# Moving the maximum's injection and the second value half within a turn, with a first attention that copies less on VectorE

## The chip, the cores and the metric

The kernel runs on one core of one Trainium2 chip. Its time is the device time of one launch in microseconds. One profiled execution gives the trace that all durations come from.

## The reference, cut to what matters

The input is 16 sequences of 256 tokens with 128 channels, in fp32. A first attention layer (16 heads of 8 channels, windows of 64 tokens, no look-back) is added to the input; then six layers of a local transformer (16 heads of 64 channels, windows of 32 tokens that also see the window before) follow on its normalised result.

```python
x = x + first_attention(layernorm(x))           # qkv, layernorm of q and k per head, softmax over 64 keys, projection
h = layernorm(x)
for i in range(6):
    a = shift_tokens(h)                          # half of the channels come from the token before
    q, k, v = split(a @ Wqkv[i])                 # 128 -> 3 x 1024
    q, k = rotary(l2norm(q) * qs), rotary(l2norm(k) * ks)
    p = softmax(8 * q @ k.T, masked to the own and the preceding window)
    h = h + (p @ v) @ Wo[i]                      # 1024 -> 128
    h = h + ffn(shift_tokens(h))                 # layernorm, 128 -> 2 x 341, a * gelu(gate), 341 -> 128
x = x + h
```

## The kernel before, in words

**First attention.** `first_attention` works on eight units of 512 tokens. Each passes through six stages (`stage_load`, `stage_qkv`, `stage_heads`, `stage_soft`, `stage_out`, `stage_norm`), and a loop over 25 steps puts the stages of several units side by side; `merge` mixes their pieces by offsets. `row_stats` takes the mean and the spread of a row with ScalarE activations that accumulate. `stage_heads` splits queries and keys into two fp16 parts (`hl`: a cast on ScalarE, the remainder on GpSimd), doubles them by a copy on VectorE, and transposes by DMA. `stage_out` multiplies probabilities with values for the two halves `c` of the rows, each half into a PSUM tile `po` of its own, divides on VectorE, and projects. `SPLIT0` gives the PSUM banks of the pools in the order `pq`, `ps`, `po`, `py`, `pt`.

**The six layers.** There are 192 tiles of 128 tokens, 32 in a layer, and the main loop makes one turn for each. A turn works on five tiles at once: the projections of tile t (`stage_p`: key halves K0 and K1, query halves Q0 and Q1, value halves V0 and V1, each three fp16 matmuls of 512 columns), the scores of t-1 (`stage_s`), the softmax of t-2 (`stage_e`), the product with the values of t-3 (`stage_v`, in two halves `mb`, below called v0 and v1) and the output product of t-5 (`stage_w`). Between a projection's matmuls stand four fp32 transposes on TensorE (`turned`): of K and Q of t-1 beside K0 to Q1, of the probabilities of t-2 beside V0 and V1. ScalarE copies four of them at a time out of PSUM. A piece of the feed-forward (`stage_f`) of an earlier group of four tiles is added to a turn.

**What sets the order.** Every stage is a generator, and `AT_*` gives the place of each of its pieces in a turn, from 0 to 1. `merge_at` sorts them, with ties going to the part that was appended first. Every matmul and transpose is pinned behind the one before (`pin`), so TensorE runs exactly in the written order. The other engines' orders come from the framework's scheduler at build time, and stand then: each engine runs its instructions in that order.

```python
AT_P = tuple(c / 6 for c in range(6))
AT_E, AT_V, AT_W, AT_S = (0.2, 0.21), (0.1, 0.45), (0.47,), (0.72,)
SPLIT = (2, 4, 2)
USE = dict(p=0, t=1, w=1, f=1, s=2)
USE_V = (1, 2)
```

So the order of a turn on TensorE before is K0, v0, K1, injection, Q0, v1, w, Q1, V0, scores, V1, with the feed-forward's pieces in between.

**The softmax.** The scores open with a mask matmul (`rowsb`, `maskb`) into two PSUM tiles, one for each parity `a` of the head, and stay in PSUM. VectorE takes their negated maxima (`nm`, L738). In the next turn `stage_e` adds these with a matmul against an identity (`identh`), the maximum's injection, and ScalarE takes the exponentials (`p`, L275).

**PSUM.** `SPLIT` gives two banks to the projections, four to transposes, output product, feed-forward and v0, and two to scores and v1. The last two banks therefore go round within a turn: exponentials read them, v1 writes them, VectorE reads v1's result (`rc` L790, `of` L791), and the mask of the next scores writes them again.

**VectorE in a turn.** Four `mc` (L643, the rotary product of a projection of K or Q), four `r` (L653, the sum of the squares that ScalarE makes, L652), two `nm`, four `rc` and four `of` (two for each value half), two `xg` (L817, the output product added to the stream), and the feed-forward's and the weight splits' (L137) operations. ScalarE's square of a projection starts after VectorE's `mc` of the same bank.

**The end.** `emit_out` transposes a finished group back on TensorE, with PSUM from the projections' two banks, adds the first residual on VectorE (L834) and stores it.

Of the kernel before, what the change touches and what calls it, by code (L numbers as in the profile page):

```python
# [10 lines left out]
F32 = mybir.dt.float32  # L11
# [3 lines left out]
AF = mybir.ActivationFunctionType  # L15
ALU = mybir.AluOpType
AX = mybir.AxisListType
# [7 lines left out]
KT = 2  # L25
LAG_S, LAG_P, LAG_V, LAG_W = 1, 2, 3, 5
AT_P = tuple(c / 6 for c in range(6))
AT_E, AT_V, AT_W, AT_S = (0.2, 0.21), (0.1, 0.45), (0.47,), (0.72,)
AT_F = ((0.86,), (0.06, 0.74, 0.88), (0.03, 0.27, 0.8), (0.1, 0.35, 0.6))
AT_L = 0.71  # L30
LOAD_AT = 6
LOAD_T = 10
SPLIT = (2, 4, 2)
SPLIT0 = (2, 2, 2, 1, 1)
USE = dict(p=0, t=1, w=1, f=1, s=2)
USE_V = (1, 2)
LQ0, LH0, LS0, LO0, LN0 = 2, 4, 6, 7, 9
# [11 lines left out]
VPRE = 16.0  # L49
# [6 lines left out]
def kernel(  # L56
# [233 lines left out]
    def mul(*args, **how):  # L290
        pin(T.matmul(*args, **how))  # L291
# [5 lines left out]
    def first_attention(p1, p2, p3, pqp, psp0, pop, pyp, ptp=None):  # L297
# [17 lines left out]
        def row_stats(xt, pre):  # L315
            mu = p3.tile([128, 4], F32, name=f"{pre}mu")
            rs = p3.tile([128, 4], F32, name=f"{pre}rs")
            sq = p3.tile([128, 128], F32, name="sq0")
            for t in range(4):
                S.activation(sq, xt[:, t], AF.Copy, scale=-1.0 / 128.0, accum_out=mu[:, t : t + 1])  # L320
            for t in range(4):
                S.activation(sq, xt[:, t], AF.Square, bias=mu[:, t : t + 1], accum_out=rs[:, t : t + 1])
            rsqrt(rs, rs, 1.0 / 128.0)
            return mu, rs
# [39 lines left out]
        def stage_load(u):  # L364
            if u:
                load_x(u)
            e = U[u]
            _, e.rs = row_stats(e.xt, "a")
            e.rv = p1.tile([128, 4], F32, name="rv")
            V.tensor_scalar(e.rv, e.rs, VPRE, None, ALU.mult)  # L370
            yield
            e.xnt = p1.tile([128, 2, 4, 128], FR, name="xnt")
            pt = ptp.tile([128, 4, 128], F32, name="pt" if ptp is not pyp else "py")
            for t in range(4):
                T.transpose(pt[:, t], e.xt[:, t], ident)
            S.copy(e.xnt[:, 0], pt)
            V.tensor_tensor(e.xnt[:, 1], pt, e.xnt[:, 0].bitcast(F32), ALU.subtract)
            G.tensor_tensor(e.xt, e.xt, bpt.unsqueeze(1).to_broadcast([128, 4, 128]), ALU.add)
            yield
# [26 lines left out]
        def stage_heads(u):  # L406
            e = U[u]
            e.hl = []
            for s in range(2):
                src = e.qk[:, :, s * 128 : s * 128 + 128].rearrange("p t (h d) -> p t h d", d=8)  # L410
                hl = p1.tile([128, 4, 16, 4, 8], HP, name=f"hl{s}")
                for t in range(4):
                    hi, lo = hl[:, t, :, 0], hl[:, t, :, 2 if s else 1]
                    S.copy(hi, src[:, t])
                    G.tensor_tensor(lo, src[:, t], hi, ALU.subtract)
                    if s:
                        V.tensor_copy(hl[:, t, :, 1:4:2], hl[:, t, :, 0:3:2])
                    else:
                        V.tensor_copy(hl[:, t, :, 2:4], hl[:, t, :, 0:2])
                tr = p2.tile([128, 4, 4, 128], HP, name=f"tr{s}")  # L420
                nc.sync.dma_start_transpose(
                    tr.rearrange("p t i q -> p (t i) q"), hl.rearrange("p t h a d -> p (t h a d)")
                )
                e.hl.append(tr)
                yield
# [41 lines left out]
        def stage_out(u, n2):  # L467
            e = U[u]
            for n in range(2):
                t = 2 * n2 + n  # L470
                pt0 = e.pt[n]
                v = v0[(4 * u + t) % NV0]
                o0 = p3.tile([128, 2, 8, 8], F32, name="o0")
                for c in range(2):
                    r = slice(64 * c, 64 * c + 64)
                    po = pop.tile([128, 8, 18], F32, name="po")
                    for gm in range(8):
                        p = gm % 4 * 2 + gm // 4
                        for q, (a, b) in enumerate(((0, 0), (0, 1), (1, 0))):
                            T.matmul(po[:, p], pt0[r, a * 8 + gm], v[r, b, p], start=(q == 0), stop=(q == 2))  # L480
                    rc = p3.tile([128, 8], F32, name="rc0")
                    V.reciprocal(rc, po[:, :, 16])
                    for hp in range(2):
                        h = slice(64 * hp, 64 * hp + 64)
                        V.tensor_tensor(
                            o0[h, c],
                            po[h, :, hp * 8 : hp * 8 + 8],
                            rc[h].unsqueeze(2).to_broadcast([64, 8, 8]),
                            ALU.mult,
                        )  # L490
                yield
                py = pyp.tile([128, 512], F32, name="py")
                T.transpose(py[:, 0:128], o0.rearrange("p c a b -> p (c a b)"), ident)
                ot0 = p3.tile([128, 128], F32, name="ot0")
                S.copy(ot0, py[:, 0:128])
                py = pyp.tile([128, 512], F32, name="py")
                for c in range(2):
                    r = slice(64 * c, 64 * c + 64)
                    for hp in range(2):
                        T.matmul(  # L500
                            py[r, 0:128],
                            ot0[r, hp * 64 : hp * 64 + 64],
                            wp[r, hp],
                            start=(hp == 0),
                            stop=(hp == 1),
                        )
                V.scalar_tensor_tensor(e.xt[:, t], py[:, 0:128], 1.0 / VPRE, e.xt[:, t], ALU.mult, ALU.add)
                yield
# [49 lines left out]
    def bank(kind):  # L558
        n = USE.get(kind, kind)
        return banks[n].tile([128, 512], F32, name=f"bank{n}")  # L560
# [47 lines left out]
    def turned(src, dst, mb):  # L608
        hold = []

        def one(m):
            if m == 0:
                hold.append(bank("t").rearrange("p (m q) -> p m q", q=128))
            flip(hold[0][:, m], src(m), ident)
            if m == 3:
                to = dst
                if isinstance(dst, Tl):
                    if mb == 0:
                        dst.pt = work.tile([128, 8, 128], F32, name="pt", bufs=1)
                    to = dst.pt  # L620
                S.copy(to[:, mb * 4 : mb * 4 + 4], hold[0])  # L621

        turns.extend((lambda m=m: one(m)) for m in range(4))

# [63 lines left out]
    def line_up(t):  # L688
        if 0 <= t - LAG_S < total:
            d = tiles[t - LAG_S]  # L690
            if d.j == 0:
                kts[0] = front.tile([128, 8, 256], F32, name="kt", bufs=KT)
            d.ktp = kts[0]
            d.kt = d.ktp[:, :, 128 - 128 * d.j : 256 - 128 * d.j]
            d.qt = front.tile([128, 8, 128], F32, name="qt", bufs=2)
            for s, dst in ((1, d.kt), (0, d.qt)):
                for hb in range(2):
                    nat = d.nat[s][hb].rearrange("p (m a) d -> p m (a d)", a=2)
                    turned(lambda m, nat=nat: nat[:, m], dst, hb)
        if 0 <= t - LAG_P < total:  # L700
            d = tiles[t - LAG_P]
            for mb in range(2):
                turned(lambda m, mb=mb: d.p[:, mb * 4 + m].rearrange("p a k -> p (a k)"), d, mb)

# [60 lines left out]
    def stage_v(t):  # L765
        d = tiles[t]
# [11 lines left out]
        for mb in range(2):  # L778
            po = [bank(USE_V[mb])[:, 0:260].rearrange("p (m d) -> p m d", d=65) for a in range(2)]
            for m in range(4):  # L780
                for s in range(4):
                    for a in range(2):
                        r = slice(64 * a, 64 * a + 64)
                        q = slice(32 * s, 32 * s + 32)
                        mm = mb * 4 + m
                        mul(po[a][q, m], d.pt[r, mm, q], vv[s, a][r, mm], start=True, stop=True)
            of = work.tile([128, 4, 2, 64], F32, name="of", bufs=2)
            for a in range(2):
                rc = work.tile([128, 4], F32, name="rc", bufs=4)
# [30 lines left out]
    def emit_out(b, nb):  # L820
        g, k = divmod(b, GB)
        n = 2 * nb
# [4 lines left out]
        yt = pool.tile([128, 12 if name == "gt" else 4, 128], F32, name=name, bufs=bufs)[:, 0:n]  # L827
        for a in range(2):
            r = slice(64 * a, 64 * a + 64)
            pm = bank("p")[:, 0:256].rearrange("p (t c) -> p t c", c=64)[:, 0:n]  # L830
            for t in range(n):
                c0 = t % 2 * 128 + a
                flip(pm[:, t], xg[g][r, k + t // 2, c0 : c0 + 128], ident[r, r])
            V.tensor_tensor(yt[:, :, r], pm, r1[:, :, r], ALU.add)  # L834
# [187 lines left out]
```

## Time and profile before

| what | value |
|---|---|
| median of three runs | 3218.96 us (3212.57 to 3219.44) |
| the profiled execution | 3213.12 us, its span 3211.3 us |
| TensorE (PE) busy | 2994.2 us, 93% |
| VectorE (DVE) busy | 2583.3 us, 80% |
| GpSimd (POOL) busy | 2510.2 us, 78% |
| ScalarE (ACT) busy | 2384.4 us, 74% |
| mean granted TensorE clock | 0.957 |

Reading it: an engine's busy time counts its instructions and not its waits. PE is TensorE's matmuls and PEld its weight loads, which overlap them. Matmuls overlap each other, so the time that one takes of the engine is the time from its start to the next one's start, not its duration. In the list of waits a row names who waited, on whom, for how many microseconds in all, how often, and the longest. In the table of stages each row gives the stretch, its length, and for PE, PEld, DVE, ACT and POOL the busy time and the number of instructions; then the granted clock, the DMA engines' busy share and GB/s. In a timeline a row is start, length, engine, line, operation, tiles and count; in square brackets stands the idle time before it and what ended it.

### The profile page before, as it was taken

Reading aid. Unit: us, or ns where it says so; the run is one execution under the profiler, and the core shown is the slowest. Engines: PE = TensorE matmul, PEld = TensorE weight load, DVE = VectorE, ACT = ScalarE, POOL = GpSimd, SP = SyncE. Lnnn points to the kernel's source line nnn. Section 1 sums busy time; section 2 is a strip of 40 time slices with the busy share of each in tenths; the row PEclk is TensorE's granted clock in tenths of the full one; section 3 lists DMA queues with packets and bytes.
Section 4 is the critical chain, followed back from the end, with each engine's and each line's share of the span. In section 5 each row is a group of like instructions: output and inputs, shape, how many; then the busy total and the mean of one; then the engine's idle time right before and its main releaser. Section 6 shows DMA issues by size and latency. Waiting matters only on the chain. (4 is left out here: it accounts for less than half of the span.)

```text
span 3211.3 us, 153330 instructions
## 1 busy us (share of the span) xinstructions
PE 2994.2 (93%) x67106; PEld 2099.0 (65%) x67106; DVE 2583.3 (80%) x4850; ACT 2384.4 (74%) x5034; POOL 2510.2 (78%) x2578
## 2 busy tenths in 40 slices
PE   4887999999999999999999999999999999999997
PEld 3655766666666666666666666666666666666664
DVE  7987888887788887788887788887788887787774
ACT  6877777777777777777777777777777777776774
POOL 5656988888888788888788888788888788887772
PEclk6558999999999999999999999999999999999998
DMA  4763545444444434444444444444444444443433
GB/s 109 134 130 86 101 96 106 89 85 88 93 95 107 87 87 88 93 95 105 89 87 86 94 96 104 89 88 84 95 98 103 89 89 81 95 93 91 89 89 71
DMA packets 622945, 302.98 MB, mean 94 GB/s; under 512 B 533446, under 2 KB 545732, under 8 KB 622276
## 3 DMA queue, kind: packets, MB, share of 16 engines
q1 hardware_dynamic: 622276, 293.18, 43.5%
q8 instruction: 528, 8.65, 1.1%
q14 instruction: 141, 1.16, 0.1%
HBM read 22.45 MB, written 4.19 MB: 8 GB/s over the span
## 5 line engine op out<-in xcount | busy, mean ns | idle before, releaser
L291 PE MATMUL bank<-wqkv,xhl 128*128 128x512 f16 x3456 | 1234.4, 380 | 10.0 <-ACT sq L652 9.3
L654 POOL TENSOR_TENSOR sum<-mc 128x512 f32<-128x512 f32 x768 | 995.8, 1300 | 230.4 <-DVE mc L643 211.3
L643 DVE TENSOR_TENSOR mc<-bank,tq 128x1024 f32<-128x1024 f32 x768 | 928.2, 1218 | 148.3 <-PE bank L294 135.4
L664 POOL TENSOR_TENSOR sum<-sum,r 128x512 f32<-128x512 f32 x768 | 796.2, 1058 | 31.9
L653 DVE TENSOR_REDUCE r<-sq 128x8 f32<-128x512 f32 x768 | 520.4, 683 | 277.4 <-ACT sq L652 267.4
L294 PE MATMUL bank<-ident,sum 128*128 128x128 f32 x3072 | 710.5, 273 | 0.0
L796 POOL TENSOR_TENSOR ohl<-of,ohl 128x512 f16<-128x512 f32 x384 | 451.7, 1176 | 211.5 <-ACT ohl L795 210.8
L652 ACT ACTIVATE sq<-bank 128x512 f32<-128x512 f32 x768 | 459.6, 608 | 160.4 <-DVE mc L643 158.7
L294 PEld LDWEIGHTS bank<-ident,sum 128*128 128x128 f32 x3072 | 432.4, 141 | 131.8 <-issue 13.9
L291 PEld LDWEIGHTS <-xhl 128*128 128x128 f16 x3456 | 337.6, 98 | 191.0 <-issue 18.5
L795 ACT CAST ohl<-of 128x512 f16<-128x512 f32 x384 | 237.8, 619 | 269.5 <-DVE of L791 266.8
L291 PE MATMUL bank<-vb,pt 64*32 64x65 f32 x6144 | 376.0, 225 | 50.9 <-ACT p L275 26.4
L291 PEld LDWEIGHTS bank<-vb,pt 64*32 64x32 f32 x6144 | 257.0, 105 | 218.6 <-ACT p L275 75.1
L294 PE MATMUL bank<-ident,p 128*128 128x128 f32 x1536 | 355.0, 273 | 0.1
L291 PE MATMUL bank<-v,pt 64*32 64x65 f32 x6144 | 312.6, 224 | 39.4 <-ACT p L275 17.8
L291 PE MATMUL bank<-vw,pt 64*32 64x65 f32 x12288 | 331.8, 225 | 1.2 <-issue 1.0
L791 DVE TENSOR_TENSOR of<-bank,rc 128x256 f32<-128x256 f32 x768 | 295.4, 416 | 1.7
L291 PE MATMUL bank<-ot,wohl 128*128 128x128 f16 x4608 | 292.0, 220 | 2.0 <-issue 1.1
L291 PEld LDWEIGHTS bank<-kt,qt 64*32 64x32 f32 x24576 | 255.4, 105 | 44.4 <-issue 44.1
L291 PE MATMUL bank<-kt,qt 64*32 64x64 f32 (+1 forms) x24576 | 283.7, 223 | 0.3 <-issue 0.2
L291 PEld LDWEIGHTS bank<-v,pt 64*32 64x32 f32 x6144 | 235.2, 105 | 70.5 <-ACT p L275 33.2
L291 PEld LDWEIGHTS <-wohl 128*128 128x128 f16 x4608 | 259.1, 98 | 21.0 <-issue 3.1
(155 smaller groups left out, 5033.9 us busy)
## 6 DMA issues: line engine op xcount, KB each, us to landing
v<-vb SPq DMA_DIRECT2D x384, 130.0 KB
vw<-vb SPq DMA_DIRECT2D x384, 130.0 KB
vw<-vb SPq DMA_DIRECT2D x576, 65.0 KB
wraw<-in_L_ffn_Wqkv_dram SPq DMA_DIRECT2D x36, 256.0 KB
wraw<-in_L_ffn_Wo_dram SPq DMA_DIRECT2D x12, 256.0 KB
ot<-ohl SPq DMA_TRANSPOSE x192
xt<-in_L_attn_x_dram SPq DMA_DIRECT2D x8, 256.0 KB
r1d<-xt SPq DMA_DIRECT2D x8, 256.0 KB
```

What stands on the lines that cost most here:

```text
L291: pin(T.matmul(*args, **how))
L294: pin(T.transpose(*args))
L643: V.tensor_tensor(prod, p4.unsqueeze(3).to_broadcast([128, 8, 2, 2, 32]), tq[:, s, d.j].unsqueeze(1).to_broadcast([128, 8, 2, 2, 32]), ALU ...
L652: S.activation(sq, pp.rearrange("p (h d) -> p h d", d=64), AF.Square)
L653: V.tensor_reduce(r[:, hb * 8 : hb * 8 + 8], sq, AX.X, ALU.add)
L654: G.tensor_tensor(mc, m2[:, :, 0], m2[:, :, 1], ALU.add)
L664: G.tensor_tensor(mc, mc, rb.unsqueeze(2).to_broadcast([128, 8, 64]), ALU.mult)
L791: V.tensor_tensor(of[:, :, a], po[a][:, :, 0:64], rc.unsqueeze(2).to_broadcast([128, 4, 64]), ALU.mult)
L795: S.copy(ohl[:, 0, h], of)
L796: G.tensor_tensor(ohl[:, 1, h], of, ohl[:, 0, h], ALU.subtract)
```

## The change

- The places in a turn: the injection and the exponentials go to 0.12 and 0.13, the value halves to 0.16 and 0.5, the output product to 0.42. The order on TensorE becomes K0, injection, v0, K1, Q0, w, Q1, v1, V0, scores, V1.
- The transposed probabilities lie in two tiles of four blocks instead of one of eight.
- `emit_out` takes its PSUM from the pool of four banks.
- The first attention: `hl` is written already doubled, by ScalarE and GpSimd, and VectorE's copies go; the second row statistics take their sums with one VectorE reduction; `rv` moves to GpSimd; the value product of both row halves goes to one PSUM tile of two banks, with the halves alternating, and one reciprocal and two products instead of two and four. The `po` pool has one buffer instead of two.

```diff
-AT_E, AT_V, AT_W, AT_S = (0.2, 0.21), (0.1, 0.45), (0.47,), (0.72,)
+AT_E, AT_V, AT_W, AT_S = (0.12, 0.13), (0.16, 0.5), (0.42,), (0.72,)
...
-SPLIT0 = (2, 2, 2, 1, 1)
+SPLIT0 = (2, 2, 1, 1, 1)
...
-            for t in range(4):
-                S.activation(sq, xt[:, t], AF.Copy, scale=-1.0 / 128.0, accum_out=mu[:, t : t + 1])
+            if pre == "a":
+                for t in range(4):
+                    S.activation(sq, xt[:, t], AF.Copy, scale=-1.0 / 128.0, accum_out=mu[:, t : t + 1])
+            else:
+                V.tensor_reduce(mu, xt, AX.X, ALU.add)
+                G.tensor_scalar(mu, mu, -1.0 / 128.0, None, ALU.mult)
...
-            V.tensor_scalar(e.rv, e.rs, VPRE, None, ALU.mult)
+            G.tensor_scalar(e.rv, e.rs, VPRE, None, ALU.mult)
...
+                hi, lo = (slice(0, 2), slice(2, 4)) if s else (slice(0, 3, 2), slice(1, 4, 2))
                 for t in range(4):
-                    hi, lo = hl[:, t, :, 0], hl[:, t, :, 2 if s else 1]
-                    S.copy(hi, src[:, t])
-                    G.tensor_tensor(lo, src[:, t], hi, ALU.subtract)
-                    if s:
-                        V.tensor_copy(hl[:, t, :, 1:4:2], hl[:, t, :, 0:3:2])
-                    else:
-                        V.tensor_copy(hl[:, t, :, 2:4], hl[:, t, :, 0:2])
+                    two = src[:, t].unsqueeze(2).to_broadcast([128, 16, 2, 8])
+                    S.copy(hl[:, t, :, hi], two)
+                    G.tensor_tensor(hl[:, t, :, lo], two, hl[:, t, :, hi], ALU.subtract)
...
-                for c in range(2):
-                    r = slice(64 * c, 64 * c + 64)
-                    po = pop.tile([128, 8, 18], F32, name="po")
...
+                both = pop.tile([128, 2, 512], F32, name="po")
+                po = both[:, :, 0:144].rearrange("p c (m e) -> p c m e", e=18)
+                for gm in range(8):
+                    p = gm % 4 * 2 + gm // 4
+                    for q, (a, b) in enumerate(((0, 0), (0, 1), (1, 0))):
+                        for c in range(2):
+                            r = slice(64 * c, 64 * c + 64)
+                            T.matmul(po[:, c, p], pt0[r, a * 8 + gm], v[r, b, p], start=(q == 0), stop=(q == 2))
...
-                    if mb == 0:
-                        dst.pt = work.tile([128, 8, 128], F32, name="pt", bufs=1)
-                    to = dst.pt
-                S.copy(to[:, mb * 4 : mb * 4 + 4], hold[0])
+                    dst.pt[mb] = work.tile([128, 4, 128], F32, name=f"pt{mb}", bufs=1)
+                    S.copy(dst.pt[mb], hold[0])
...
-                        mul(po[a][q, m], d.pt[r, mm, q], vv[s, a][r, mm], start=True, stop=True)
+                        mul(po[a][q, m], d.pt[mb][r, m, q], vv[s, a][r, mm], start=True, stop=True)
...
-            pm = bank("p")[:, 0:256].rearrange("p (t c) -> p t c", c=64)[:, 0:n]
+            pm = bank("t")[:, 0:256].rearrange("p (t c) -> p t c", c=64)[:, 0:n]
```

More of the change, by code (lines that the diff above doesn't have):

```diff
@@ L473, in stage_out @@
                 o0 = p3.tile([128, 2, 8, 8], F32, name="o0")
-                for c in range(2):
-                    r = slice(64 * c, 64 * c + 64)
-                    po = pop.tile([128, 8, 18], F32, name="po")
[L477 to L490, printed above, removed]
+                both = pop.tile([128, 2, 512], F32, name="po")
[6 more added lines that the diff above has]
+                            T.matmul(po[:, c, p], pt0[r, a * 8 + gm], v[r, b, p], start=(q == 0), stop=(q == 2))
+                rc = p3.tile([128, 2, 8], F32, name="rc0")
+                V.reciprocal(rc, po[:, :, :, 16])
+                for hp in range(2):
+                    h = slice(64 * hp, 64 * hp + 64)
+                    V.tensor_tensor(
+                        o0[h],
+                        po[h, :, :, hp * 8 : hp * 8 + 8],
+                        rc[h].unsqueeze(3).to_broadcast([64, 2, 8, 8]),
+                        ALU.mult,
+                    )
                 yield
@@ L615, in one @@
             if m == 3:
-                to = dst
                 if isinstance(dst, Tl):
-                    if mb == 0:
-                        dst.pt = work.tile([128, 8, 128], F32, name="pt", bufs=1)
-                    to = dst.pt
-                S.copy(to[:, mb * 4 : mb * 4 + 4], hold[0])
+                    dst.pt[mb] = work.tile([128, 4, 128], F32, name=f"pt{mb}", bufs=1)
+                    S.copy(dst.pt[mb], hold[0])
+                else:
+                    S.copy(dst[:, mb * 4 : mb * 4 + 4], hold[0])
         turns.extend((lambda m=m: one(m)) for m in range(4))
@@ L701, in line_up @@
             d = tiles[t - LAG_P]
+            d.pt = [None, None]
             for mb in range(2):
```

## The prediction

> **What bounds the kernel now.** First the page's totals and its forty slices: TensorE is busy at nine tenths from the fifth slice on, and its clock is at half before that.
>
> ```profile
> PE 2994.2 (93%) x67106; PEld 2099.0 (65%) x67106; DVE 2583.3 (80%) x4850; ACT 2384.4 (74%) x5034; POOL 2510.2 (78%) x2578
> ...
> PE   4887999999999999999999999999999999999997
> ...
> PEclk6558999999999999999999999999999999999998
> ```
>
> Second, busy time by stage (first attention, six layers, the end of the last layer):
>
> ```profile
> 12.00:272.00 260.00, 190.82 (x3005) 141.49 (x3004) 218.12 (x548) 188.91 (x556) 144.98 (x128) 0.51 0.61 118
> 272.00:2992.00 2720.00, 2608.05 (x59998) 1825.04 (x59997) 2217.96 (x4015) 2050.82 (x4186) 2232.85 (x2279) 1.00 0.44 93
> 2992.00:3212.00 220.00, 189.82 (x4089) 128.42 (x4088) 143.03 (x278) 136.11 (x261) 128.10 (x130) 0.95 0.38 82
> ```
>
> The layers are 85% of the time. PE (the first column) is idle there for only 112 us, so TensorE sets the pace, with VectorE and GpSimd at 82%. In the first attention VectorE (third column) is the fullest, 218 of 260 us. Third, the waits of the layers: most of PE's idle time ends with the exponential of the maximum-injected scores.
>
> ```profile
> PEld bank L291 <- ACT p L275: 98.0, 223, 0.7
> PE bank L291 <- ACT p L275: 38.1, 152, 0.4
> PE bank L291 <- ACT pt L621: 20.5, 44, 0.5
> ```
>
> The first two are the second value half (v1), which takes over the two score banks when the exponentials have read them; the third is the first half (v0) waiting for transposed probabilities. Fourth, the timeline of one turn around the next use of those banks, VectorE and then TensorE:
>
> ```profile
> 1528.02 1.22 DVE L643 TENSOR_TENSOR mc<-bank,tq 128x1024 f32<-128x1024 f32 x1
> 1529.15 0.67 DVE L653 TENSOR_REDUCE r<-sq 128x8 f32<-128x512 f32 x1
> 1529.75 0.24 DVE L790 RECIPROCAL rc<-bank 128x4 f32<-128x4 f32 x2
> 1529.96 0.69 DVE L653 TENSOR_REDUCE r<-sq 128x8 f32<-128x512 f32 x1
> 1530.56 0.74 DVE L791 TENSOR_TENSOR of<-bank,rc 128x256 f32<-128x256 f32 x2
> 1531.22 0.58 DVE L817 SCALAR_TENSOR_TENSOR xg<-bank,xg 64x128 f32<-64x128 f32 x2
> 1531.84 1.22 DVE L643 TENSOR_TENSOR mc<-bank,tq 128x1024 f32<-128x1024 f32 x1
> ```
> ```profile
> 1531.79 0.39 PE L291 MATMUL bank<-maskb,rowsb 64*128 64x512 bf16 x2
> ```
>
> VectorE runs without a gap and some 1.3 us behind TensorE. The two `of` (v1's results out of the score banks) end at 1531.30; the next scores, which open with the mask matmul in the same banks, start at 1531.79. Over 171 turns that slack is 0.49, 0.78, 1.63 and 0.96 us in the four kinds of turn (by what the feed-forward does in them; call them A centre and mean, B gelu, C second product, D nothing), 0.97 on average. It is what the change spends.
>
> **The layers, part by part.** *The reordering on TensorE.* It runs in the written order, so a turn becomes: K0, injection, v0, K1, Q0, w (the output product), Q1, v1, V0, scores, V1. No matmul is added. What goes: v1's wait for the exponentials, as those now stand two projections earlier and v1 one later. By start-to-start times a value half takes 0.793 us unhindered; v1 takes 1.083 on average, and after a transpose its first matmul comes 0.23 us late, so 0.29 x 181 + 0.23 x 135 = 84 us. v0 takes 1.071 and is some 0.14 late; the injection ahead of it (0.43 us) hides about 0.22 of that a turn, 42 us. *The two probability tiles* are in that: v0 then waits for the first copy alone.
>
> *What is late next.* In the built order VectorE has, between v0's first reciprocal and v1's last `of`, one more `mc` (Q1's) than before, both `xg` of w, and in kind B one more `r`. With start-to-start times of this trace (`mc` 1.13, `r` 0.60, `rc` 0.09, `of` 0.34, `xg` 0.29, feed-forward ops 0.58 to 0.75) the four kinds add to 8.1, 9.1, 9.2 and 7.6 us, against 6.4, 6.4, 7.9 and 5.8 before: 1.85 more. The scores' mask waits for that `of` by semaphore, and nothing on TensorE may pass it. TensorE in contrast has only V0 (1.09) between v1 and the scores, where it had w, Q1 and V0 (3.5). So a slack of 0.97 meets 1.85 of added VectorE work.
>
> One turn of kind D walked through, from the mask at 0. Scores 1.73, V1 and K0 1.09 each: 3.9. Injection 0.43: 4.33. v0's last matmul starts at 5.2, readable at 5.5. ScalarE: two exponentials 4.5 to 5.6, then K0's square to 6.15. VectorE: `rc` to 5.7, `r` (waits for that square) to 6.8, `of` to 7.5, two `mc` to 9.8, `r` 10.4, `xg` 11.0, `r` 11.6, Q1's `mc` 12.7, `rc` 12.9, `of` 13.6. Mask at 13.65; TensorE alone would have been there at 12.2, and before the turn took 12.42. So +1.2. The same walk gives A 16.7 for 14.81 (+1.9: the mean's matmul and both exponentials come before K0's square), B 16.4 for 16.83 (-0.4: its gelu waits, 1.2 us at v0, shrink, as VectorE's last `r` comes sooner after the mask and the table load with it), C 17.2 for 16.43 (+0.8). Sum 3.5 us in four turns. The weight splits (0.70 each) stand inside this stretch in a third to a half of the turns of B, C and D: 0 to 1.0 us in four turns, I take 0.5. 4.0 x 46.5 groups of four = **+186 us**. From below: the waits for squares inside VectorE's stretch (0.04, 1.0, 0.5 and 0.3 us before) could all vanish, 1.8 in four turns, and the splits cost nothing: 1.7 x 46.5 = +79. From above: the splits in full and 0.4 more in B: 4.9 x 46.5 = +228. The middle value is taken, as it is the one whose order is the built one.
>
> Queues: behind the waiting mask stand V1, K0 and the injection on PE; VectorE's two `nm` follow `of` and wait through the scores (1.73). On GpSimd one `ohl`, and on SP's queue the DMA transpose behind it, come some 2 us later in a turn; the transpose takes 4.28 us in the chain and w reads it two turns (30 us) later, so 0; without that cover it would be up to 4.3 us a turn.
>
> *A stall and the clock.* At 3016.6 to 3020.0 PE was busy 1.82 of 3.40 us, and the clock stood at 0.50 for the next 3.4. D's stall of 1.5 us leaves about 56% of such a stretch, so this is near; one trip lengthens scores (2.02 for 1.45 there) and V1, about 0.8 to 1.2 us. I take none, and 100 us in a rival. The Trainium skill ("TensorE: Matmul & The Clock Gate", "What's actually happening") says the clock falls after an idle window of about 3.4 us; by that no stall of 1.5 us would lower it, while the row here fell with half a window idle, so the row decides.
>
> **The first attention.** VectorE loses 64 copies (14.5 + 13.3 us), 8 `rv` (567 ns, 4.5), half its reciprocals (12.6 to about 7) and of its 128 products of 219 ns (28.0) keeps 64 of double size (nearest row 285 ns: 18.2); it gains 8 reductions of 0.68 (5.5). Net -42 of 218. ScalarE: 64 casts double (0.294 to 0.416, +7.8), 32 sums go (-15.8). GpSimd: 64 subtractions double (0.431 to 0.657, +14.5), 16 small ops of 0.25 (+4). The value product alternates row halves into two banks and its accumulator is single: the next one waits for three VectorE ops (about 0.8 us) that the old pair of banks hid in part; against that, alternate halves may overlap. -10 to +25 for the two. VectorE is the fullest, PE next (191 at half clock), ScalarE at 189: two thirds of 42 should show, **-28 us**, between -45 and +10.
>
> The Trainium skill ("SBUF — State Buffer", "SBUF: two separate sides") speaks against part of this: a GpSimd op locks the port it shares with VectorE for its whole length. Rows agree that VectorE is held up (`rv` takes 155 ns at best, 1521 at worst); by the rule up to the 18.5 us that GpSimd gains would come back.
>
> **The end.** Output transposes drew from two banks and now from four. Their wait (9.4 us in six pieces on `gt` L834) goes: **-9**, between -10 and 0.
>
> **Sum.** The profiled execution took 3213.1 (span 3211.3 and 1.8 around it; the median of the three runs is 6 above, 0.2%, which is about what a measurement of this kernel can tell from no change). 3213 + 186 - 28 - 9 = 3362, said as **3360**; own range 3270 (79 in the layers, -22 elsewhere) to 3440.
>
> **Rivals.** *Faster: VectorE keeps up.* If v1's `of` ends before V0 does, no wait replaces the one removed: 3213 - 126 - 37 = 3050, or about 3130 with half of a wait. For it: 112 us of PE idle, and ScalarE's waits do shrink. Against it: VectorE's stretch must shrink from 7.6 to 9.2 us to below TensorE's 7.0 (7.6 in B, 9.6 in C); only C manages. Its chance is 0.22. *Slower still: the clock falls* in half the turns, 93 x 1.1 = 100, 3460; it decides once a stall passes about 1.6 us; 0.08. *A small loss:* the lower bound in the layers with the full -54 elsewhere, 3240; 0.10. *Nothing to see:* 0.03, the two signs cancelling. The forecast has 0.57.
>
> The range runs from 3150 to 3440: above it lie 0.08, below it about half of the faster case. Slower 0.75, within 0.2% 0.03, faster 0.22.
>
> **What would show it.** Right: PEld or PE at the mask (`rowsb`) idle for over 150 us, ended by VectorE's `of` (53 us on the page before, 19 of it ended by VectorE); `ACT p` gone from the waits of the value matmuls; VectorE idle before `nm` for about 1.7 us a turn; turn D about 13.6 us. Wrong: slack left between `of` and the mask, or PE idle below 112 us in the layers. First attention: the layers' clock reaches 1.0 before 255 us instead of 272.

## The result, and the profile after

The changed kernel takes 3476.39 us (median of four runs, 3471.23 to 3479.43); the kernel before took 3217.44 beside it. The ratio is 1.0806 [1.0785, 1.0826]: slower, as forecast, by 259 us where 147 were forecast, and beyond the range's upper end of 3440. The profiled execution took 3471.23 (span 3469.5).

The page's totals and slices come first, in the form shown of before:

```profile
PE 3015.7 (87%) x67106; PEld 2082.2 (60%) x67106; DVE 2593.1 (75%) x4690; ACT 2407.8 (69%) x4968; POOL 2532.8 (73%) x2594
...
PE   5878888998888898988899888899888898889987
...
PEclk9959999999999999999999999999999999999999
```

No engine works more than 1% longer than before, in a span that is 8% longer; TensorE's slices, nines before, are now mostly eights. The work has hardly grown: the engines wait for each other more. The table of stages shows the same stretches (the last one begins later, as the kernel is longer):

```profile
12.00:255.00 243.00, 171.52 (x3005) 122.88 (x3004) 191.29 (x388) 186.21 (x492) 161.84 (x142) 0.84 0.66 127
272.00:2992.00 2720.00, 2409.99 (x54665) 1663.68 (x54665) 2045.30 (x3650) 1887.68 (x3791) 2028.79 (x2064) 0.99 0.38 84
3200.00:3469.00 269.00, 231.57 (x5079) 156.80 (x5060) 180.96 (x345) 167.26 (x326) 164.40 (x167) 0.97 0.39 84
```

In 2720 us of the layers TensorE now works 2410 us instead of 2608. Which waits took their place, in the list of waits of that stretch:

```profile
PEld L291 <- DVE of L793: 317.0, 329, 3.2
...
DVE nm L740 <- PE bank L291: 230.5, 148, 2.6
PE bank L291 <- DVE of L793: 217.2, 174, 2.9
...
DVE r L654 <- ACT sq L653: 112.1, 122, 2.3
...
PE bank L291 <- ACT sq L653: 64.7, 88, 1.9
```

The rows of `ACT p`, which led the list before, are gone. In their place TensorE waits for VectorE's `of` (PEld and PE wait at the same time, so the two are not added), and then, in a different place, 64.7 us for ScalarE's squares, which had 9 us before; 59.5 of these stand before Q1 in turns of kind A and D. The third row is the counterpart: VectorE waits for the scores that it held up. The costliest groups of the page say where TensorE waits:

```profile
L291 PE MATMUL bank<-maskb,rowsb 64*128 64x512 bf16 x384 | 139.5, 388 | 252.2 <-DVE of L793 245.6
...
L740 DVE TENSOR_REDUCE nm<-bank 128x8 f16<-128x512 f32 x384 | 247.3, 686 | 273.2 <-PE bank L291 270.4
```

`maskb,rowsb` is the mask matmul that opens the scores, the only use of those names. One turn of kind C shows the pair, VectorE first, then TensorE:

```profile
1546.73 1.23 DVE L644 TENSOR_TENSOR mc<-bank,tq 128x1024 f32<-128x1024 f32 x1
1547.87 0.24 DVE L792 RECIPROCAL rc<-bank 128x4 f32<-128x4 f32 x2
1548.03 0.66 DVE L137 SCALAR_TENSOR_TENSOR wqkv<-wraw,wqkv 128x512 f16<-128x512 f32 x1
1548.61 0.75 DVE L793 TENSOR_TENSOR of<-bank,rc 128x256 f32<-128x256 f32 x2
1549.27 0.68 DVE L654 TENSOR_REDUCE r<-sq 128x8 f32<-128x512 f32 x1
1551.23 1.29 DVE L740 TENSOR_REDUCE nm<-bank 128x8 f16<-128x512 f32 x2 [1.29 <-PE bank L291]
```

```profile
1549.08 0.72 PE L291 MATMUL bank<-maskb,rowsb 64*128 64x512 bf16 x2 [1.03 <-DVE of L793]
```

TensorE has been idle for 1.03 us when the mask starts, released by the first of the two `of`. VectorE has by then run without a gap through `mc`, `rc`, a weight split (L137) and `of`; the slack of 0.49 us in the timeline of before has become a wait. In all four kinds of turn the mask now follows the end of the `of` that releases it by 58 ns: the mask has two matmuls, one for each parity, and each follows the `of` of its own bank. One `r` further on VectorE is out of work and waits 1.29 us for the scores.

Three marks divide the span: the first mask, the last of the 192 masks, the end.

| kernel (profiled execution, us) | first mask at | first to last mask | rest |
|---|---|---|---|
| before | 287.5 | 2867.9 | 56.0 |
| after | 272.7 | 3142.2 | 54.5 |
| after, with before's places | 274.4 | 2856.9 | 54.9 |

So the first attention gave back 15 us, the layers lost 274, and the end is 1.5 us shorter, which can't be told from nothing: over the runs below the rest varies from 52 to 59 us. The third row is the first experiment: it splits the 274 into 285 for the new places and -11 for the two probability tiles and the output transposes, by one profiled execution of each kernel.

### The profile page after: what moved, and what is told of

It is laid out like the page before. It is cut to its first block, busy times and chain, and to the rows that moved or that the text cites. A ratio compares the mean times of both kernels' runs of the same rounds, so it can differ in the third digit from the quotient of the medians.

```text
span 3469.5 us, 153217 instructions
## 1 busy us (share of the span) xinstructions
PE 3015.7 (87%) x67106; PEld 2082.2 (60%) x67106; DVE 2593.1 (75%) x4690; ACT 2407.8 (69%) x4968; POOL 2532.8 (73%) x2594
## 4 chain that ended last, share of the span: by engine, by line
PE 37%; DVE 28%; ACT 15%; POOL 11%; issue 5%; DMA 2%; SPq 1%; ACTq 0%; POOLq 0%; DVEq 0%
PE bank L291 31%; DVE mc L644 10%; DVE r L654 6%; PE bank L294 6%; POOL sum L655 5%; DVE of L793 5%; ACT p L275 4%; ACT sq L653 3%; POOL ohl L798 3%; POOL sum L665 2%; ACT ohl L797 2%; DVE rc L792 1%; DVE xg L819 1%; DVE xnhl L868 1%; ACT gt L275 1%
## 5 line engine op out<-in xcount | busy, mean ns | idle before, releaser
L291 PE MATMUL bank<-wqkv,xhl 128*128 128x512 f16 x3456 | 1253.0, 385 | 105.1 <-ACT sq L653 77.3
L671 ACT COPY vb<-bank 128x512 f32<-128x512 f32 x384 | 224.3, 584 | 335.6 <-PE bank L291 330.6
L291 PEld LDWEIGHTS <-xhl 128*128 128x128 f16 x3456 | 339.9, 98 | 187.3 <-issue 26.7
L740 DVE TENSOR_REDUCE nm<-bank 128x8 f16<-128x512 f32 x384 | 247.3, 686 | 273.2 <-PE bank L291 270.4
L294 PE MATMUL bank<-ident,p 128*128 128x128 f32 x1536 | 363.2, 279 | 0.1
L291 PE MATMUL bank<-maskb,rowsb 64*128 64x512 bf16 x384 | 139.5, 388 | 252.2 <-DVE of L793 245.6
L291 PEld LDWEIGHTS bank<-vb,pt 64*32 64x32 f32 x6144 | 247.7, 105 | 134.6 <-issue 72.8
L291 PE MATMUL bank<-vw,pt 64*32 64x65 f32 x12288 | 326.8, 225 | 0.0
L291 PE MATMUL bank<-vb,pt 64*32 64x65 f32 x6144 | 318.2, 223 | 1.0 <-ACT pt L620 1.0
L291 PE MATMUL bank<-v,pt 64*32 64x65 f32 x6144 | 309.1, 225 | 0.0
L622 ACT COPY qt<-bank 128x512 f32<-128x512 f32 x384 | 224.8, 586 | 110.1 <-PE bank L294 103.7
L291 PEld LDWEIGHTS <-wohl 128*128 128x128 f16 x4608 | 272.0, 98 | 48.0 <-issue 29.3
L291 PE MATMUL bank<-ot,wohl 128*128 128x128 f16 x4608 | 290.1, 220 | 3.1 <-DMA ot<-ohl 1.9
```

The source lines that it names most:

```text
L294: pin(T.transpose(*args))
L622: S.copy(dst[:, mb * 4 : mb * 4 + 4], hold[0])
L671: S.copy(vb[:, :, hb * 4 : hb * 4 + 4, 0:64], pp.rearrange("p (m a d) -> p a m d", a=2, d=64),)
L740: V.tensor_reduce(nm, pss[a], AX.X, ALU.max, negate=True)
```

## The experiments

Theory: the new places let v1, which ends in the score banks, come so late that VectorE's `of` is the last thing the scores wait for. Rivals: the earlier injection costs the time; the parts beside the places do; the clock does. All edits are against the changed kernel unless said otherwise, and all runs have an interval against the kernel before.

### The places, taken out and put in alone

The changed kernel with before's places:

```diff
-AT_E, AT_V, AT_W, AT_S = (0.12, 0.13), (0.16, 0.5), (0.42,), (0.72,)
+AT_E, AT_V, AT_W, AT_S = (0.2, 0.21), (0.1, 0.45), (0.47,), (0.72,)
```

> The changed kernel with the four place tuples of before, so all of the change but the reordering. Theory (the reordering makes the mask matmul of the scores wait for v1's `of` on VectorE, and that is the loss): the wait of `rowsb` for `of` falls from 604 us of PEld idle to below 40, and the time is that of before less what the first attention and the end gain: 3217 - 19 - 9, about 3190 us (3170 to 3215). Rival (the first attention's or the two tiles' part of the change costs time): above 3250.

The kernel before with the new places, the same lines the other way round in its own file:

> The kernel before with the new places alone. Theory: the whole loss of the layers, 1.48 us in each of some 190 turns, without the gains elsewhere: 3217 + 281, about 3500 us (3470 to 3520). Rival (the single tiles and the reordering only together): within 100 us of before.

Measured: 3192.81, ratio 0.9930 [0.9915, 0.9945], and 3508.47, 1.0915 [1.0899, 1.0932]. The places alone cost 291 us on the kernel before and 284 on the changed one; everything else together gains 25 to 32. With before's places TensorE's idle time at the mask is 2.2 us instead of 252:

```profile
L291 PE MATMUL bank<-maskb,rowsb 64*128 64x512 bf16 x384 | 75.5, 388 | 2.2 <-ACT xg L527 2.2
```

(The 604 us that the expectation names are the waits of PE and PEld added.) This version is 0.7% faster than the kernel before, a small gain, but outside the interval.

### The early injection alone, the late v1 alone

```diff
-AT_E, AT_V, AT_W, AT_S = (0.12, 0.13), (0.16, 0.5), (0.42,), (0.72,)
+AT_E, AT_V, AT_W, AT_S = (0.12, 0.13), (0.16, 0.45), (0.47,), (0.72,)
```

> The changed kernel with the second value half and the output product back at 0.45 and 0.47 and the injection still first: K0, injection, v0, K1, Q0, v1, w, Q1, V0, scores, V1. VectorE then has v1's `of` ahead of w's `xg` and Q1's `mc`. Theory: no wait at the mask, none of v1 for the exponentials: 3190 - 84 - 42, about 3065 us (3040 to 3140). Rival (it is the early injection that harms, as the exponentials hold up ScalarE's squares and with them the projections' banks and VectorE's `r`): over 3250.

```diff
-AT_E, AT_V, AT_W, AT_S = (0.12, 0.13), (0.16, 0.5), (0.42,), (0.72,)
+AT_E, AT_V, AT_W, AT_S = (0.2, 0.21), (0.1, 0.5), (0.42,), (0.72,)
```

> The changed kernel with the injection and the first value half at their old places (0.2, 0.21 and 0.1), and the second half late (0.5) after the output product (0.42). Theory (the late second half puts `of` behind Q1's `mc` and w's `xg`, and the mask waits): the loss stays, less what early exponentials take from ScalarE's squares (2.2 to 3.4 us in four turns): 3310 to 3370 us. Rival (the loss is mainly the early injection's): under 3250.

Measured: 3253.13, 1.0122 [1.0105, 1.0139], and 3385.14, 1.0519 [1.0503, 1.0534]. The first denied the theory of a gain of some 130 us: the early injection by itself costs 60 us over before's places. The second put most of the loss on v1, a little more than expected; its row of the mask:

```profile
L291 PE MATMUL bank<-maskb,rowsb 64*128 64x512 bf16 x384 | 140.9, 397 | 202.0 <-DVE of L793 196.8 <-ACT xg L527 2.1 <-DVE b1t L203 1.2
```

The four corners, in us:

| | injection at 0.2 | injection at 0.12 |
|---|---|---|
| v1 ahead of w | 3192.8 | 3253.1 |
| v1 behind w and Q1 | 3385.1 | 3476.4 |

v1's place costs 192 to 223 us, the injection's 60 to 91. What the early injection costs with v1 early is to be seen in the waits of that run:

```profile
PE bank L291 <- ACT sq L653: 59.7, 68, 1.3
...
PE bank L291 <- ACT gt L858: 31.9, 37, 1.6
```

The first row is TensorE at a projection whose bank ScalarE's square has not yet read; with before's places it had 3.7 us. Of the 59.7 us, 52 fall in turns of kind B, nearly all before Q0, which takes the bank of K0 again. ScalarE now has both exponentials ahead of the square of K0, and the projections go round on two banks, so a later square holds up a later projection. The second row (6.1 us with before's places) is a matmul of the feed-forward in kind A, which waits for a square of ScalarE's too. The mask still waits 24.8 us for `of`, in kind A alone. The clock is not it: the layers of this run have no window at half clock.

### v1 in banks of its own

If it is the shared banks that make v1's place dear, then v1 in the pool of four, where v0 is, should cost little wherever it stands:

```diff
-USE_V = (1, 2)
+USE_V = (1, 1)
```

> The changed kernel in the changed order, with the second value half in the pool of four banks instead of the scores' two. The mask then follows the exponentials in its banks and not v1's `of`; VectorE's order and load stay. Theory (the shared bank turns VectorE's lag into TensorE's wait): the mask's wait goes, the layers fall back by most of 1.5 us a turn: 3080 to 3200 us. Rival (VectorE's load or the projections' wait for squares bounds the turn in any case): 3350 to 3470.

The same edit with before's places, and with before's injection and the late v1:

> The changed kernel with the places of before and the second value half in the pool of four banks. Theory: v1 no longer waits for the exponentials (about 84 us before), the scores' banks have a whole turn; the ring of four must now serve two more uses: 3110 to 3193 us. Rival (the ring of four becomes the wait): above 3193.

> The changed kernel with the injection at its old place, the second half late and in the pool of four banks. Against the run with other banks and the early injection (3241) this shows what the early injection alone costs where no mask waits. Theory (the early exponentials stand before ScalarE's squares and hold up the projections' banks): 3130 to 3200 us. Rival (the squares are late because VectorE's `mc` is late, whatever the injection's place): 3230 to 3260.

Measured: 3240.52, 1.0081 [1.0066, 1.0096]; 3197.07, 0.9934 [0.9919, 0.9949]; 3193.82, 0.9925 [0.9911, 0.9940]. The mask's row in the first of them:

```profile
L291 PE MATMUL bank<-maskb,rowsb 64*128 64x512 bf16 x384 | 74.9, 387 | 2.1 <-ACT xg L527 2.1
```

The wait is gone, and the layers fall from 3142 to 2909 us: 233 of the 274 hung on the sharing. With banks of its own a late v1 costs nothing on balance (3193.8 against 3197.1: kind B is 1.36 us shorter, A, C and D are 0.42, 0.26 and 0.48 longer), while the early injection still costs 47 us (3240.5 against 3193.8). Its row, of the run with both moves and then of the run with the late v1 alone:

```profile
PE bank L291 <- ACT sq L653: 118.4, 138, 1.9
```

```profile
PE bank L291 <- ACT sq L653: 66.1, 95, 1.6
```

The difference between the rows is 52 us, and 50 of them stand before Q0 in turns of kind B, where the run with the late v1 alone has next to none. The trace shows why: with the early injection an exponential is the last thing that ScalarE does before K0's square in all 176 turns compared, and in kind B that square starts 3.74 us after the end of K0's `mc` instead of 2.25 (0.75, 0.62 and 0.35 in A, C and D instead of 0.27, 0.03 and 0.03). Kind B is 1.24 us longer by the early injection, the other three together are not. This is a second new wait, which the forecast did not have. A row of waits is not a price by itself, though: with before's places and the other banks this row has 8.6 us, and the late v1 raised it to 66.1 at no cost in time. The first run missed its expectation (3080 to 3200) by 40 us.

The second run answers another question. With before's places and v1 in other banks no matmul waits for the exponentials any more, and the time does not move (3197.1 against 3192.8), which is where its rival put it (above 3193). The waits for exponentials that the prediction had counted as 84 us of gain gave nothing back: TensorE arrives 0.2 us earlier at v1 (9.73 us into a turn of kind A against 9.93) and 0.67 earlier at w, is 0.34 ahead at Q1 (12.21 against 12.55), and at the mask 0.05 (14.77 against 14.82). Two reasons are open. The other engines' work had not become less; and the ring of four serves two more uses a turn, with new waits of TensorE in place of the 38.5 us that it had for `ACT p`: 17.2 us for `gt` L888 (6.5 before this edit) and 31.7 us for nothing that the profile shows (3.2).

### The scores behind V1

One more projection (1.09 us) between v1 and the mask gives VectorE that much more time:

```diff
-AT_E, AT_V, AT_W, AT_S = (0.12, 0.13), (0.16, 0.5), (0.42,), (0.72,)
+AT_E, AT_V, AT_W, AT_S = (0.12, 0.13), (0.16, 0.5), (0.42,), (0.9,)
```

> The changed kernel with the scores at 0.9 instead of 0.72, so behind V1: one more projection (1.09 us) between v1 and the mask. Theory (the mask waits for VectorE's lag): the wait shrinks by up to 1.09 us in each of 190 turns, of which some comes back as the injection waits for `nm`, now with only K0 in between: 3280 to 3380 us. Rival (VectorE is the bound of the whole turn): within 40 us of 3476.

Measured: 3321.69, 1.0320 [1.0303, 1.0337]. `PE bank L291 <- DVE of L793` falls from 217 to 15 us, but 192.7 us stand at `ACT sq`: 70 before Q1 in kinds A and D, 45 before Q0 in kind B, and 72 before V1, which had none. Why the squares come late for V1 was not tested. The wait moved, and only 155 of 284 us came back.

### One more reduction on VectorE

If VectorE sets the time from v1 to the mask, a reduction that nobody reads must show there in full, and be partly hidden with before's places. A second sum of K1's squares:

```diff
                 V.tensor_reduce(e.r[s][:, hb * 8 : hb * 8 + 8], sq, AX.X, ALU.add)
+                if s == 1 and hb == 1:
+                    again = front.tile([128, 8], F32, name="again", bufs=2)
+                    V.tensor_reduce(again, sq, AX.X, ALU.add)
```

> The changed kernel with one reduction more on VectorE in each turn: K1's squares are summed a second time into a tile that nobody reads, which adds 0.60 us to VectorE's stretch before v1's `of`. Theory (VectorE's lag is TensorE's wait at the mask): nearly all of it shows in time, 0.60 x 190 = 114: 3476 + 114 = 3590 us (3560 to 3620). Rival (the turn is set by the banks and ScalarE, not by how much VectorE does): under 3520.

> The same extra reduction with the places of before (without it: 3193 us). Theory: `of` has a slack of 0.5 to 1.6 us before the mask there, and VectorE is 82% busy, so most of the 0.60 us a turn is hidden: 3193 to 3235 us. Rival (VectorE's load is the bound in either order): about 3300.

Measured: 3610.54, 1.1225 [1.1206, 1.1244], and 3250.89, 1.0110 [1.0095, 1.0125]. With the new places the op costs 134 us, or 0.70 us in each of 192 turns, its own length of 0.68 (`r` in the timeline above) on average. The kinds share it unevenly (1.45, 0.83, 0.42 and 0.34 us in A to D), for a reason that was not looked into; the mask follows `of` by 56 ns in all of them. The mask's rows, new places and then before's:

```profile
L291 PE MATMUL bank<-maskb,rowsb 64*128 64x512 bf16 x384 | 142.8, 413 | 326.3 <-DVE of L796 324.5 <-ACT xg L527 1.7
```

```profile
L291 PE MATMUL bank<-maskb,rowsb 64*128 64x512 bf16 x384 | 93.0, 388 | 13.5 <-DVE of L796 11.8 <-ACT xg L527 1.7
```

Idle time at the mask rises by 74 us in the one and stays small in the other. With before's places the op still costs 58 us, 0.30 a turn, between what either theory gave: VectorE was not free there, only not alone in setting the pace.

### The first attention

Before's value product, with its two `po` tiles, put back into the version with before's places:

```diff
-SPLIT0 = (2, 2, 1, 1, 1)
+SPLIT0 = (2, 2, 2, 1, 1)
...
-                both = pop.tile([128, 2, 512], F32, name="po")
...
+                for c in range(2):
+                    r = slice(64 * c, 64 * c + 64)
...
```

> The changed kernel with the places of before and the value product of the first attention as before (two tiles of one bank, two buffers). In all runs with the change the first mask starts some 15 us earlier than in the kernel before, where I had expected 28. Theory (the single two-bank accumulator gives back a part of what the copies bring): the first mask some 5 to 13 us earlier still, 3180 to 3190 us. Rival (VectorE's work was not what the first attention waits for): the first mask within 3 us of 274, or later, 3190 us and over.

Measured: 3198.26, 0.9948 [0.9933, 0.9963]. The first mask comes at 280.3 us instead of 274.4: the new product gains 6 us instead of costing 5 to 13. That leaves 7 of the 13 us between 287.5 and 274.4 to the copies, sums and `rv`.

### The late v1 in one turn of four

The longest turn, kind B, has TensorE waiting for a gelu. Before's places, and in turns of kind B alone the late v1 in the pool of four:

```diff
-    def stage_v(t):
+    def stage_v(t, use=USE_V):
...
+                if (t - LAG_W - 3) % 4 == 2 and lag == LAG_V:
+                    parts.append(((0.1, 0.5), stage_v(t - lag, (1, 1))))
+                    continue
+                if (t - LAG_W - 3) % 4 == 2 and lag == LAG_W:
+                    places = (0.42,)
```

> The changed kernel with the places of before, save in every fourth turn, the one whose early part holds the last gelu and the table load (kind B): there the second value half is late (0.5), the output product at 0.42, and both value halves use the pool of four banks. With other banks and the old injection kind B took 15.54 us against 16.75, the other kinds 0.2 to 0.4 more than with the old places. If the kinds are independent, 1.2 us less in 46 turns: 3193 - 55 = 3138 us, 0.975 of before (3130 to 3165). Rival (the time is only pushed into the turn after, whose scores have less ahead of them): within 10 us of 3193.

Measured: 3189.98, 0.9918 [0.9901, 0.9934]. Turn B falls from 16.82 to 16.27 us on average, but C rises from 16.23 to 16.55 and D from 12.44 to 12.60; the work was pushed on. This time, that of before's places (3192.8) and that of the late v1 in other banks (3193.8) are the best, and they are not told apart.

## Why the prediction was right in sign and wrong in size

**Right.** The chain: `of`, not TensorE, ends last before the mask. The signs given for it came: TensorE idle at the mask for 252 us (over 150 said), 245.6 of it ended by `of`; `ACT p` gone; VectorE waiting 1.4 us a turn before `nm` (270.4 over 192 turns; 1.7 said). Only turn D, said to take 13.6 us, took 14.84. The rival in which VectorE keeps up fell with them: it needs slack behind `of`, and there are 58 ns. v1's place with the shared banks as the cause is shown by the corners and by the banks of its own; that VectorE's length sets it is shown by the 58 ns and by the reduction that cost its full length on average.

**The step that failed: VectorE's stretch from v0's first `rc` to the mask.** From mask to mask:

| kind | before | walked | measured after |
|---|---|---|---|
| A, centre and mean | 14.81 | 16.7 | 17.05 |
| B, gelu | 16.83 | 16.4 | 17.29 |
| C, second product | 16.43 | 17.2 | 17.28 |
| D, nothing | 12.42 | 13.65 | 14.84 |

The prediction has 34.0 us for this stretch in the four kinds together, and 0.5 for weight splits: 34.5. Counted to the second matmul of the mask, which follows the last `of`, it measured 36.7 (8.69, 9.94, 9.74, 8.36). What is left of the walked turns, 29.95 us from the mask to `rc`, measured 29.7: TensorE's and ScalarE's part was right in the sum (in D, `rc` came 5.95 us after the mask where the walk has 5.5). So the term that was mis-sized is VectorE's stretch, by 2.2 us in four turns; times 46.5 groups of four that is some 100 us. The layers missed by 88 us (+186 forecast, +274 measured, or +285 for the places alone).

What makes the 2.2 us: the ops of the stretch were priced well, 34.1 us without the splits. The splits took 1.2 us instead of 0.5. VectorE stands idle for 1.2 us (0.08, 0.32, 0.27, 0.53), of which the walk spells out only the wait of D, although the lower bound takes 1.8 off for such waits: about 0.65 of it ends with ScalarE's squares, in C and D, and 0.3 in B with TensorE, at a projection's `mc`. The last 0.2 are the 58 ns between `of` and the mask, four times.

In B a gain was forecast, through a gelu that comes sooner. It came out as a loss, 17.29 against 16.83: there too the mask follows `of` by 58 ns, and B has the largest share of the splits, 0.57 us a turn.

**A wait that was not in the sum.** Projections wait for squares, 64.7 us in the layers. In kind A w comes 9.70 us and Q1 12.07 us after the mask; where w runs unhindered, 1.35 us lie between them. These waits are inside the 285, and they come with the late v1: with before's injection they are 64.3 us in the same places. How much of them also lies inside VectorE's stretch (TensorE's delay at Q1 delays Q1's `mc`, which stands ahead of v1's `of`) was argued and not measured.

**The credit for removed waits.** 126 us of waits at v1 and v0 were taken to be time on the path. In the sum the walk of the turns superseded that figure, but the faster rival stood on it. The 84 us for exponentials, removed by other banks, gave back nothing. The 42 us at v0 were not tested in this way: in that run 15.8 of the 20.4 us of waits for transposed probabilities remain.

**The clock.** This rival held in part. The layers of the changed kernel have 23 windows of 3.41 us at half clock, 78 us (one before), 22 of them in the turns compared here. Turns with such a window are longer than others of their kind by 2.2 us (B, 3 turns), 2.3 (C, 8), 1.3 (D, 4) and 1.4 (A, 7): 40 us of the 285. That is an upper bound, as long stalls themselves bring the window about. Nothing tests it alone. The run with one more reduction has 69 stretches at half clock, 270 us; in the turns that neither kernel has one in, its op still costs 0.63 us on average.

**The first attention** gave 15 us for 28, inside the bounds of -45 to +10. VectorE's busy time there fell by 27 us (218.1 in 260 us, 191.3 in 243) and ScalarE's by 3, while GpSimd gained 17. The value product's rewrite, put at -10 to +25 as a cost, gained 6. So VectorE's lost copies are worth 7 us, not two thirds of 42; with VectorE at 191, ScalarE at 186 and TensorE at 172 of 243 us, another engine was close behind. Which of them takes over was not tested.

**The end** gave 1.5 us for 9, within what the rest varies by from run to run.

## What to carry to other kernels

Where a PSUM bank goes from one user to the next, the engine that empties it is in the path with its whole backlog: count every instruction that stands in its queue between the fill and the last read, waits on third engines included, against what the matmul engine has left to do until it needs the bank again. A removed wait need not be a gain; here waits counted as 84 us went and nothing came back, while the turn's work on the other engines stayed and other waits grew. When moving a step on one engine, list what then stands ahead of whom on every other: the earlier injection, which puts two exponentials ahead of a square on ScalarE, cost 47 to 91 us with no work added.

## What the runs showed of the hardware

Value matmuls that alternate between the two halves of the rows, into two banks, overlap. In the first attention, before and after, at half clock:

```profile
L480 PE MATMUL po<-v,pt 64*128 64x18 f16 x1344 | 45.9, 173 | 10.7 <-DMA pt<-ph 10.4 <-DVE o L485 0.3
```

```profile
L482 PE MATMUL po<-v,pt 64*128 64x18 f16 x1513 | 33.7, 174 | 19.8 <-DMA pt<-ph 16.4 <-DVE o L487 3.3
```

One takes as long (173 and 174 ns), but the busy time per recorded matmul falls from 34 ns (45.9/1344) to 22 (33.7/1513). In the run with before's value product it is 32 (46.3/1440).

The granted clock of the page can mislead: the changed kernel's slices show 0.9 in the first attention, where before had 0.5. The matmuls there are no faster:

```profile
L387 PE MATMUL pq<-w0hl,xnt 128*128 128x384 f32 x91 | 38.6, 560 | 24.2 <-DVE v L393 24.2
```

```profile
L391 PE MATMUL pq<-w0hl,xnt 128*128 128x384 f32 x91 | 39.2, 573 | 23.7 <-DVE v L397 23.4
```

560 ns before, 573 after: both ran at half clock. The first clock event in this trace is at 172 us, and what lies before it is filled in. The mean granted clock (0.975 after, 0.957 before) is therefore not a comparison of the two.

Windows of 3.41 us at half clock come with short stalls: 23 in the changed kernel's layers, where TensorE's wait for `of` is 1.25 us on average (217.2/174) and its longest idle time of any kind 2.87, and 69 stretches with one more reduction; with before's places there is none. In the 3.41 us ahead of each of the 23, TensorE was busy for 25 to 55% of the time; of the windows that no half clock followed, the least busy had 45%. The Trainium skill ("TensorE: Matmul & The Clock Gate", "What's actually happening") lets the clock fall after an idle window of about 3.4 us. Here TensorE is never idle for that long, so the measurement decides.

A doubled write is not free: ScalarE's cast into `hl` went from 294 to 407 ns and GpSimd's subtraction from 431 to 687 ns, close to the 416 and 657 worked out from neighbouring rows.
